# Six planned layers of a Trainium2 kernel: unread identity products where the planner expects TensorE to wait, and the delta rule's output in two groups of products

## The chip, the cores and the metric

The kernel runs on one core of one Trainium2 chip. The time is the device time of one execution in microseconds, from runs without the profiler; the profile is one further execution, taken by the hardware profiler. The core's engines are TensorE (PE in the profile, with its weight loads as PEld), VectorE (DVE), ScalarE (ACT), GpSimd (POOL) and SyncE (SP), which issues transfers. TensorE reads SBUF and writes PSUM[...].

## The reference

Eight sub-layers, each added to the residual stream x after a layer norm. x has 8 sequences of 256 positions and 128 channels in the kernel's layout.

```python
for f in (gated_delta_rule, windowed_attention_ffn, plucker_attention,
          ternary_ffn, flash_attention, mixture_of_experts,
          bidirectional_mamba, int8_ffn):
    x = x + layernorm(f(layernorm(x)))
```

The change touches the first of them most. Its core, for each of 16 heads with 64 key and 128 value channels, is the recurrence

```python
S = S * exp(g_t)                      # S: 64 x 128 a head
delta = (v_t - k_t @ S) * b_t
S = S + outer(k_t, delta)
o_t = (q_t * 64 ** -0.5) @ S
```

after which o is normed, gated and projected. Everything is fp32.

## The kernel before

**The delta rule in chunks.** `l0_attn` works on units of one sequence and eight heads (two units a sequence, 16 in all), each cut into two chunks of 128 positions, c = 0 and c = 1. For each chunk `prepare` makes scaled and transposed keys and queries, `decays` the decay factors E, `products` the matrices M (keys with keys) and, in E's place, the masked products of queries and keys. `inverse` inverts the triangular matrices of the eight heads by levels, in products of 64x64 tiles (L739 to L812) with evacuations between them. `outputs` forms what remains. Its output step is at L859 to L867: in a PSUM tile of 128 x 2 x 512 fp32 each head h has a region of 128 columns, at bank r = h // 4 and place p = h % 4. L863 adds `Q[:, h, :]` times `dl[:, h, :]` (128 contraction rows, inside the chunk); for c = 1, L865 adds `T2` times the state `St` that chunk 0 left (64 contraction rows: heads of r = 0 in the lower half of the partitions, those of r = 1 in the upper). The two alternate, head by head. After the step, L870 squares the result on ScalarE. L826, earlier in `outputs`, multiplies another half of `T2` with the same `St`, all eight heads in one go.

**The planner.** The first six layers are written as tasks, each a Python generator that yields between steps. `Turns.run` keeps a clock for each engine and a price for each instruction, and each time takes the step that could start first; so the order in which the instructions of all six layers are issued is fixed by the planner's clock when the program is built. On the chip an engine takes its instructions in that order and waits by semaphores. A step that names "ps" in its `yield` needs one of four PSUM slots (`ps`, 4 KB a partition each[...]) and two classes of SBUF slots (`4k`, `2k`, 25 each). `S.leave` gives a slot back to the planner at the step's planned end.

Parts that the change reads:

- `issued` is called for every instruction; it prices it, moves `clock[engine]` and `now`. For TensorE, `matmul` does so: 1.7 ns a column for fp32, 0.85 for a transpose, 0.43 for bf16; `tiles` holds when each 32x32 tile of the array is free, and a change between half and whole rows or columns (`mode`) waits for all of them and 150 ns (`SWITCH`).
- `starts` remembers, for each step of each generator's code, on which engine its first instruction ran when the step was first met.
- `ready`, set in `run`, is the time at which the step's task and its slots are ready in the planner's clock.
- `ps()` takes the PSUM tile for a step; nearly all of the 54 calls stand right before the step's first product.
- `k.ident16` is the identity in bf16, used before in the mask products of L670, L1081 and L1348, which multiply it with a mask repeated over 512 or 256 columns.

**After the six layers** come the Mamba layer `l3_attn` and the last FFN `l3_ffn`, in an order written out by hand. They start with L1898 and use neither the planner nor its slots.

The tile framework makes an instruction wait for the last readers of a buffer that it writes. A product's instruction, and any ahead of it in TensorE's queue that writes the same slot, therefore waits until the slot's last reader is done.

Some names in the profile: `Z` and `XY` are the inverse's tiles (L763; L339 and L341 are `evac` on ScalarE and VectorE), `E` in L863 is `Q`, `S` is `St`, `T` is `T2` there.

Of the kernel before, what the change touches and what calls it, by code (L numbers as in the profile page):

```python
# [16 lines left out]
P = 128  # L17
# [145 lines left out]
class Ctx:  # L163


    def __init__(self, tc, I, es):
        self.tc, self.nc, self.I = tc, tc.nc, I
        self.const = es.enter_context(tc.tile_pool(name="const", bufs=1))
        self.small = es.enter_context(tc.tile_pool(name="small", bufs=8))
        self.turn = 0  # L170
# [96 lines left out]
def over(ap, n, axis):  # L267

    a = ap.unsqueeze(axis)
    s = list(a.shape)  # L270
    s[axis] = n
    return a.to_broadcast(s)


class Turns:
# [2 lines left out]

    HOP, SWITCH = 150.0, 150.0

    def __init__(self, k, es, slots):
        self.nc = k.nc
        self.pools = {
            c: es.enter_context(k.tc.tile_pool(name="turns_" + c, bufs=n, **({"space": PSUM} if c == "ps" else {"side": "right"})))
            for c, n in slots.items()
        }
        self.slots = {c: [0.0] * n for c, n in slots.items()}
        self.clock, self.starts, self.users = {}, {}, {}  # L290
        self.tables = self.mode = None
        self.tiles = {}
        self.tasks = []
        self.now = self.queue = 0.0

    def add(self, name, after, steps):
        self.tasks.append((len(self.tasks), list(after), name, steps))
# [32 lines left out]
        return self.pools[c].tile(shape, F32, name=name, tag=c)  # L330

    def ps(self):
        return self.tile("ps", [P, 2, 512], "ps")

    def evac(self, out, in_):

# [34 lines left out]
    def issued(self, ins):  # L371

        e, op = str(ins.engine), ins.opcode
        aps = [a for a in list(ins.outs) + list(ins.ins) if hasattr(a, "bass_ap")]
        if not aps or "DMA" in op or "SP" in e:
            return
        n = max(self.size(a) for a in aps)
        if "PE" in e:
            self.matmul(ins, aps)
            return  # L380
        elif "Pool" in e:
            t = 350.0 + (1.6 if n > 64 else 160.0 if "pow" in str(getattr(ins, "op", "")) else 2.0) * n
        elif "Act" in e:
            t, f = 190.0 + 0.83 * n, str(getattr(ins, "func", ""))
            table = next((x for x in ("Silu", "Gelu", "Sqrt") if x in f), "Exp" if "Exp" in f or "Tanh" in f else self.tables)
            if table != self.tables:
                self.tables, t = table, t + 1283.0
        else:
            t = (165.0 if op != "TensorScalarPtr" else 205.0) + 1.03 * n
        start = max(self.clock.get(e, 0.0), self.ready if e == self.engine else self.now + self.HOP)  # L390
        self.clock[e] = start + t
        self.now = max(self.now, start + t)
        self.first = self.first or (e, None)
        self.engine = e

    def run(self):
        ends, live, todo = {}, [], self.tasks
        self.tasks = []
        hook = self.issued
        self.nc.push_inst_callback(hook)  # L400
        while live or todo:
            for task in [t for t in todo if all(a in ends for a in t[1])]:
                todo.remove(task)
                order, after, name, steps = task
                live.append([order, max([ends[a] for a in after], default=0.0), {}, name, steps, 0])
            best = None
            for task in live:
                order, ready, needs, _, steps, at = task
                if any(len(self.slots[c]) < n + spare for c, (n, spare) in needs.items()):
                    continue  # L410
                for c, (n, _) in needs.items():
                    ready = max(ready, sorted(self.slots[c])[n - 1])
                engine, mode = self.starts.get((steps.gi_code, at)) or (None, None)
                free = self.clock.get(engine, 0.0)
                if mode:
                    free = max([free] + list(self.tiles.values())) + self.SWITCH * (mode != self.mode)
                key = (max(ready, free), order)
                if best is None or key < best[0]:
                    best = key, ready, task
            assert best, [(t[3], t[2]) for t in live]  # L420
            _, ready, task = best
            for c, (n, _) in task[2].items():
                for i in range(n):
                    self.slots[c].remove(min(self.slots[c]))
            self.now = self.ready = ready
            self.engine = self.first = None
            needs = next(task[4], self)
            self.starts.setdefault((task[4].gi_code, task[5]), self.first)
            task[5] += 1
            if needs is self:  # L430
                live.remove(task)
                ends[task[3]] = self.now
            else:
                task[1], task[2] = self.now, {}
                for c in (needs or "").split():
                    c, _, spare = c.partition("+")
                    n, most = task[2].get(c, (0, 0))
                    task[2][c] = n + 1, max(most, int(spare or 0))
        self.nc.remove_inst_callback(hook)
# [24 lines left out]
def l0_attn(k, S, before, soon):  # L464
# [12 lines left out]
    nc, x, sm = k.nc, k.x, k.sm  # L477
    R2, H4, C2 = range(2), range(4), range(2)
    HALF = (slice(0, 64), slice(64, 128))
# [27 lines left out]
    def gates(n):  # L507

        yield "2k+5 ps"
        gt = gts[n] = S.tile("2k", [P, 7, 4, 16], "gates")  # L510
        ps, xT = S.ps(), xTs[n]
        beta, g, eG, eGd, z, u, acc = (gt[:, i] for i in range(7))
        for j in H4:
# [16 lines left out]
        nc.vector.scalar_tensor_tensor(g, acc, -1.0, over(k.l0a_alog, 4, 1), ALU.mult, ALU.mult)  # L530
        yield "ps"
        ps, gf = S.ps(), g.rearrange("p i h -> p (i h)")
        nc.tensor.matmul(ps[:, 0, 0:64], k.upto, gf, start=True, stop=True)
        nc.tensor.matmul(ps[:, 0, 64:128], k.ones, gf, start=True, stop=True)
# [282 lines left out]
    def outputs(h2, b, c):  # L817
        heads = "p r (s t) -> p (r s) t"
        v, Q, Yf, T2, xT = vs[h2, b][c], Es[h2, b, c], Yfs[h2, b, c], T2s.get((h2, b)), xTs[b // 2]
        if c:  # L820
            St = Ss[h2, b]
            yield "ps"
            ps = S.ps()
# [7 lines left out]
        ps = S.ps()  # L831
# [3 lines left out]
        dl = S.tile("4k", [P, 8, P], "dl")  # L835
        S.evac(dl.rearrange("p h t -> p (h t)"), ps.rearrange("p r c -> p (r c)"))
        S.leave("ps")
        if c == 0:
            yield "ps"
            ps = S.ps()  # L840
# [4 lines left out]
            St = Ss[h2, b] = S.tile("2k", [P, 4, P], "S")  # L845
# [4 lines left out]
        ps = S.ps()  # L850
# [7 lines left out]
        S.leave("ps")  # L858
        yield "ps"  # L859
        ps = S.ps()  # L860
        for h in range(8):
            r, p = divmod(h, 4)
            nc.tensor.matmul(ps[:, r, p * P:(p + 1) * P], Q[:, h, :], dl[:, h, :], start=True, stop=c == 0)  # L863
            if c:
                nc.tensor.matmul(ps[:, r, p * P:(p + 1) * P], T2[HALF[r], 0, p, :], St[HALF[r], p, :], start=False, stop=True)  # L865
        if c:
            S.leave("4k", "2k")  # L867
        yield
        osq = Q
        nc.scalar.activation(osq.rearrange("p h t -> p (h t)"), ps.rearrange("p r c -> p (r c)"), AF.Square)  # L870
# [12 lines left out]
        ps = S.ps()  # L883
# [31 lines left out]
    for n in H4:  # L915
        add(("n", n), before(n) + [own("x", 2 * n - 4)] * (n > 1), normed(n))
        add(("g", n), [own("n", n)], gates(n))
        for b in (2 * n, 2 * n + 1):

            add(("y", b), [own("n", n)] + [own("x", b - 3)] * (b > 2), room_for(b))  # L920
            for h2 in R2:
                u = 2 * b + h2
                prev = [own("o", (u - UNITS) % 2, (u - UNITS) // 2, 0)] if u >= UNITS else []
                add(("p", h2, b), [own("n", n), own("y", b)] + prev, project(h2, b, 0))
                for c in C2:
                    add(("r", h2, b, c), [own("p", h2, b), own("g", n)], prepare(h2, b, c))
                    add(("d", h2, b, c), [own("r", h2, b, c)], decays(h2, b, c))
                    add(("m", h2, b, c), [own("d", h2, b, c)], products(h2, b, c))
                for c in C2:
                    add(("i", h2, b, c), [own("m", h2, b, c)], inverse(h2, b, c))  # L930
                add(("v", h2, b), [own("m", h2, b, 1)], project(h2, b, 2))
                for c in C2:
                    after = [own("i", h2, b, c), own("v", h2, b)] + [own("o", h2, b, 0)] * c + [own("o", 0, b, c)] * h2
                    add(("o", h2, b, c), after, outputs(h2, b, c))
            add(("x", b), [own("o", h2, b, c) for h2 in R2 for c in C2], result(b))
# [1296 lines left out]
```

## Time and profile before

| | us |
|---|---|
| median of 3 runs (lowest to highest) | 4478.55 (4474.95 to 4483.94) |
| the profiled execution's own time | 4480.55 |
| its span, first to last instruction | 4478.8 |

| engine | busy us | share of the span | instructions |
|---|---|---|---|
| PE | 3675.4 | 82% | 54864 |
| PEld | 2916.3 | 65% | 54864 |
| DVE | 2973.7 | 66% | 4244 |
| POOL | 2723.5 | 61% | 2023 |
| ACT | 2582.6 | 58% | 4531 |

A view by stretch gives the busy time of each engine between two times. The granted clock is the share of TensorE's full clock that the throttle let through, a mean over the stretch. A group's line gives its kernel line, engine, operation, what it writes and reads by tile names, and how many; a source view adds shortest, median and longest duration in ns. Ends of products are modelled, so from one start to the next is the safer measure of what one costs. A wait's line says which engine's instruction waited for which, with the total, the number of waits and the longest. In a timeline, the brackets hold the idle time before an instruction and what ended it.

### The profile page before, as it was taken

Reading aid. Unit: us, or ns where it says so; the run is one execution under the profiler, and the core shown is the slowest. Engines: PE = TensorE matmul, PEld = TensorE weight load, DVE = VectorE, ACT = ScalarE, POOL = GpSimd, SP = SyncE. Lnnn points to the kernel's source line nnn. Section 1 sums busy time; section 2 is a strip of 40 time slices with the busy share of each in tenths; the row PEclk is TensorE's granted clock in tenths of the full one; section 3 lists DMA queues with packets and bytes.
Section 4 is the critical chain, followed back from the end, with each engine's and each line's share of the span. In section 5 each row is a group of like instructions: output and inputs, shape, how many; then the busy total and the mean of one; then the engine's idle time right before and its main releaser. Section 6 shows DMA issues by size and latency. Waiting matters only on the chain. (4 is left out here: it accounts for less than half of the span.)

```text
span 4478.8 us, 124521 instructions
## 1 busy us (share of the span) xinstructions
PE 3675.4 (82%) x54864; PEld 2916.3 (65%) x54864; DVE 2973.7 (66%) x4244; ACT 2582.6 (58%) x4531; POOL 2723.5 (61%) x2023
## 2 busy tenths in 40 slices
PE   5888888787888887889998987578887887888886
PEld 4676677676776665556555555367776876777774
DVE  6565666555556565663346676659888987987995
ACT  3434444444434454554434544388978887898883
POOL 5564556647555444441123334569988987988993
PEclk8989989898999988998898988789989999999997
DMA  1000000000000000000000000023323332333331
GB/s 54 3 2 2 3 2 3 2 2 2 9 21 3 20 11 5 8 23 15 6 1 1 5 1 1 10 79 106 100 89 95 106 98 82 105 101 89 104 111 30
DMA packets 98676, 168.86 MB, mean 38 GB/s; under 512 B 16699, under 2 KB 26582, under 8 KB 98006
## 3 DMA queue, kind: packets, MB, share of 16 engines
q1 hardware_dynamic: 98134, 160.89, 12.1%
q8 instruction: 431, 7.06, 0.6%
q14 instruction: 111, 0.91, 0.1%
HBM read 153.51 MB, written 2.10 MB: 35 GB/s over the span
## 5 line engine op out<-in xcount | busy, mean ns | idle before, releaser
L2069 POOL TENSOR_TENSOR hc<-h,Cs 128x1024 f32<-128x1024 f32 x480 | 1127.7, 2378 | 123.1 <-DVE h L2067 112.7
L2067 DVE TENSOR_TENSOR_SCAN h<-dA,ps_h 128x1024 f32<-128x1024 f32 x480 | 1069.7, 2271 | 122.7 <-PE ps_h L2061 39.0
L2046 ACT ACTIVATE dA<-dt,A 128x512 f32<-128x512 f32 x1024 | 684.7, 714 | 176.3 <-DVE h L2067 150.8
L2079 PE MATMUL ps_y<-w_c_ident,hc 128*128 128x128 f32 x4096 | 569.0, 283 | 131.7 <-POOL hc L2069 102.6
L2079 PEld LDWEIGHTS ps_y<-w_c_ident,hc 128*128 128x128 f32 x4096 | 462.2, 144 | 185.1 <-POOL hc L2069 175.7
L2043 ACT ACTIVATE sT<-dtxT,B 128x256 f32<-128x256 f32 x1024 | 451.3, 495 | 4.3 <-PE ps_h L2061 4.3
L569 DVE SCALAR_TENSOR_TENSOR acc<-ps,w_l0a_conv,acc 128x253 f32<-128x253 f32 (+2 forms) x768 | 310.6, 471 | 76.1 <-ACT acc L563 76.0
L2059 PE MATMUL ps_h<-dB,dtxTt 64*64 64x64 f32 x16384 | 305.5, 225 | 45.2 <-DVE h L2067 34.6
L2059 PEld LDWEIGHTS ps_h<-dB,dtxTt 64*64 64x64 f32 x16384 | 270.0, 138 | 99.2 <-DVE h L2067 46.3
L2061 PE MATMUL ps_h<-w_c_ident,sT 128*128 128x128 f32 x2048 | 280.5, 282 | 61.3 <-DVE h L2067 35.8
L2061 PEld LDWEIGHTS ps_h<-w_c_ident,sT 128*128 128x128 f32 x2048 | 241.8, 146 | 79.1 <-DVE h L2067 32.9
L721 POOL TENSOR_TENSOR Ps<-M,w_c_levels 128x512 f32<-128x512 f32 x192 | 240.6, 1272 | 85.9 <-DVE M L695 83.0
L339 ACT COPY XY<-ps 128x1024 f32<-128x1024 f32 (+1 forms) x132 | 124.5, 948 | 249.9 <-PE ps L786 235.6
L220 POOL TENSOR_SCALAR ln_rs<-ln_mv 128x4 f32<-128x4 f32 (+1 forms) x84 | 21.0, 251 | 397.9 <-DVE ln_mv L218 334.8
L779 PE MATMUL ps<-Z,XY 64*64 64x64 f32 x4608 | 188.7, 238 | 65.8 <-DVE Z L763 58.4
L779 PEld LDWEIGHTS ps<-Z,XY 64*64 64x64 f32 x4608 | 158.0, 148 | 84.1 <-DVE Z L763 45.1
L786 PE MATMUL ps<-XY,Z 64*64 64x64 f32 x5120 | 187.6, 237 | 4.0 <-issue 4.0
L760 PE MATMUL ps<-XY,Ps 64*64 64x64 f32 x5120 | 121.2, 234 | 75.2 <-DVE gate L880 15.9
L786 PEld LDWEIGHTS ps<-XY,Z 64*64 64x64 f32 x5120 | 164.8, 149 | 3.4 <-issue 3.4
L760 PEld LDWEIGHTS ps<-XY,Ps 64*64 64x64 f32 x5120 | 102.7, 144 | 92.2 <-issue 59.2
L563 ACT ACTIVATE acc<-ps,w_l0a_conv 128x256 f32<-128x256 f32 x256 | 100.2, 474 | 99.5 <-PE ps L557 80.6
L763 DVE TENSOR_TENSOR Z<-ps,w_c_ident 128x512 f32<-128x512 f32 x160 | 107.4, 683 | 73.0 <-PE ps L760 72.2
(456 smaller groups left out, 8716.8 us busy)
## 6 DMA issues: line engine op xcount, KB each, us to landing
Cs<-cd SPq DMA_DIRECT2D x512, 256.0 KB, 3.3
dtxTt<-dtxT SPq DMA_DIRECT2D x32, 128.0 KB, 3.9
wk<-in_l0a_w SPq DMA_DIRECT2D x8, 256.0 KB, 5.2
w_h<-in_l1f_h SPq DMA_DIRECT2D x4, 512.0 KB, 5.2
w_l2a<-in_l2a_w SPq DMA_DIRECT2D x3, 512.0 KB, 3.6
w_l0a_wg<-in_l0a_wg SPq DMA_DIRECT2D x1, 1024.0 KB
w_qk<-in_l0f_wqkv SPq DMA_DIRECT2D x2, 512.0 KB, 3.7
cv<-in_l3a_m_conv SPq DMA_DIRECT2D x2, 512.0 KB, 4.2
```

Of the source, the lines that this page charges most:

```text
L569: nc.vector.scalar_tensor_tensor(acc[:, n, s:L], p4[:, n, 0:L - s], conv[:, h2, 4 * j + n, 3 - s:4 - s], acc[:, n, s:L], ALU.mult, ALU.add,)
L721: nc.gpsimd.tensor_tensor(t, M[:, :, 0:64], over(k.l0a_levels[:, n, :], 8, 1), ALU.mult)
L760: nc.tensor.matmul(ps[to, a, at(j)], Ps[own, h, :], XY[own, t, at(i)], start=True, stop=True)
L779: nc.tensor.matmul(ps[own, a, at(j)], XY[rows, t, at(i)], Z[rows, za, at(zj)], start=True, stop=True)
L786: nc.tensor.matmul(ps[to, a, at(4 + j)], Z[rows, za, at(zj)], XY[rows, t, at(i)], start=True, stop=True)
L2043: nc.scalar.mul(st["s"][:, j], o["dtxT"][:, j], o["B"][:, j, n:n + 1])
L2046: nc.scalar.activation(dA[:, :, ec, :], by_seq(o["dt"][:, ec, :]), AF.Exp, scale=w["A"][:, ec, n:n + 1])
L2059: nc.tensor.matmul(ps[q, b, ec, j * 64:(j + 1) * 64], o["dtxTt"][rows, j, ec, q], dB[rows, j, :], start=True, stop=True)
L2061: nc.tensor.transpose(ps[:, j // 2, ec, j % 2 * P:(j % 2 + 1) * P], st["s"][:, j, ec, :], k.ident)
L2067: nc.vector.tensor_tensor_scan(h.rearrange(flat), st["dA"].rearrange(flat), st["in"].rearrange(flat), 0.0, ALU.mult, ALU.add)
L2069: (nc.vector if on_v else nc.gpsimd).tensor_tensor(st["hc"], h, over(by_seq(st["C"]), 2, 2), ALU.mult)
L2079: nc.tensor.matmul(o["py"][:, 2 * b + j, ec, :], st["hc"][:, b, ec, j * P:(j + 1) * P], k.ident, start=first, stop=n == N - 1, is_transpos ...
```

## The change

Two edits.

`Turns.ps`: before a step runs, `run` now notes in `expected` the engine that `starts` holds for it. If that is TensorE, `ps` computes how long TensorE would wait in the planner's clock, from the end of its last planned product to `ready`. For each 220 ns of it beyond 1500 ns (`IDLE`) it emits one bf16 product of the identity with the identity repeated four times, 128 x 512, into the first bank of the tile just taken. Nothing reads it; the step's own products write over it. While these are emitted `filling` is set, and `issued` leaves them out of the planner's clock.

`outputs`: for c = 1 the eight products of L865 now come first, in one group, place by place and the two row halves beside each other; then the eight products of L863. The accumulation flags change with it: a bank is started by its first product only, and `S.leave` of the two tiles moves up to stand between the groups.

```diff
-    HOP, SWITCH = 150.0, 150.0
+    HOP, SWITCH, IDLE = 150.0, 150.0, 1500.0
...
-        self.nc = k.nc
+        self.nc, self.k = k.nc, k
...
+        self.filling = False
...
     def ps(self):
-        return self.tile("ps", [P, 2, 512], "ps")
+
+
+        ps = self.tile("ps", [P, 2, 512], "ps")
+        if self.expected == "EngineType.PE":
+            gap = self.ready - max([self.clock.get("EngineType.PE", 0.0)] + list(self.tiles.values()))
+            self.filling = True
+            for _ in range(int((gap - self.IDLE) / 220.0)):
+                self.nc.tensor.matmul(ps[:, 0, :], self.k.ident16, over(self.k.ident16, 4, 1), start=True, stop=True)
+            self.filling = False
+        return ps
...
-        if not aps or "DMA" in op or "SP" in e:
+        if self.filling or not aps or "DMA" in op or "SP" in e:
             return
...
             self.engine = self.first = None
+            self.expected = (self.starts.get((task[4].gi_code, task[5])) or (None,))[0]
             needs = next(task[4], self)
...
         ps = S.ps()
+        if c:
+            for p in H4:
+                for r in R2:
+                    nc.tensor.matmul(ps[:, r, p * P:(p + 1) * P], T2[HALF[r], 0, p, :], St[HALF[r], p, :], start=p == 0, stop=False, skip_group_check=True)
+            S.leave("4k", "2k")
         for h in range(8):
             r, p = divmod(h, 4)
-            nc.tensor.matmul(ps[:, r, p * P:(p + 1) * P], Q[:, h, :], dl[:, h, :], start=True, stop=c == 0)
-            if c:
-                nc.tensor.matmul(ps[:, r, p * P:(p + 1) * P], T2[HALF[r], 0, p, :], St[HALF[r], p, :], start=False, stop=True)
-        if c:
-            S.leave("4k", "2k")
+            nc.tensor.matmul(ps[:, r, p * P:(p + 1) * P], Q[:, h, :], dl[:, h, :], start=c == p == 0, stop=True, skip_group_check=True)
         yield
```

## The prediction

> **What bounds the kernel now.** I read three views in this order: the page's slices, busy time by stretch, and the groups and waits of TensorE. The last product of the six planned layers starts at 2887.45 us (timeline of PE), so I cut the span there.
>
> ```profile
> 0.00:2888.00 2888.00, 2401.09 (x31360) 1807.02 (x31360) 1666.29 (x3348) 1282.28 (x2168) 1362.79 (x1319) 0.90 0.03 8
> 2888.00:4478.80 1590.80, 1274.33 (x23504) 1109.33 (x23504) 1307.44 (x896) 1300.32 (x2363) 1360.67 (x706) 0.94 0.31 92
> ```
>
> The columns after the length are PE, PEld, DVE, ACT, POOL busy, granted clock, DMA. In the first stretch PE is busy for 83% and the next engine (DVE) for 58%: TensorE bounds it, with 472 us of idle in 270 gaps over 0.15 us, which I added up from the trace. The second stretch (the Mamba layer and the last FFN, on POOL at 86%) is not touched by the change; I take its 1591 us as fixed.
>
> The granted clock of 0.90 is a mean over two states. In these windows around one idle time (same columns, width first) it is 1.00 or 0.50:
>
> ```profile
> 437.60:441.00 3.40, 3.40 (x53) 2.79 (x56) 3.40 (x9) 1.44 (x4) 3.40 (x3) 1.00 0.00 0
> 441.00:444.40 3.40, 0.71 (x50) 0.57 (x40) 1.36 (x4) 1.14 (x2) 3.23 (x3) 1.00 0.00 0
> 444.40:447.80 3.40, 0.00 (x0) 0.00 (x0) 2.22 (x5) 0.00 (x0) 3.40 (x4) 0.50 0.00 0
> 447.80:451.20 3.40, 1.27 (x47) 1.30 (x50) 3.40 (x7) 0.00 (x0) 3.40 (x4) 0.50 0.02 5
> 451.20:454.60 3.40, 2.99 (x50) 2.80 (x45) 3.40 (x9) 0.00 (x0) 3.40 (x4) 0.50 0.00 0
> 454.60:458.10 3.50, 3.50 (x110) 3.07 (x109) 3.50 (x10) 1.99 (x2) 2.57 (x3) 1.00 0.02 5
> ```
>
> One window with PE busy for 0.71 of 3.40 us is followed by half clock; it goes only after a window with 2.99. Over the record of the clock up to 2888 us I counted 80 half-clock periods, 597 us in all, with PE busy for 466 us of them. The window before such a period was busy for less than half in 69 cases; of 583 windows at full clock that stayed there, 3 were. Products stretch in proportion: two 128x512 bf16 products with the identity start 0.216 us apart at full clock, 0.427 at half. At full clock the 466 us would take 233: that is all there is to win from the clock.
>
> **Part 1: the output with grouped products.** For the second half of a sequence (c = 1) L863 and L865 alternate, 8 products each, and an fp32 product is two instructions:
>
> ```profile
> L865 PE MATMUL ps<-S,T x256: 272/373/579, 198.4 to 1548.5; 64*128 64x128 f32 x128
> L826 PE MATMUL ps<-S,T x256: 272/272/373, 185.1 to 1528.4; 64*128 64x128 f32 x128
> ```
> ```profile
> 284.23 0.49 PE L865 MATMUL ps<-S,T 64*128 64x128 f32 x2
> 284.65 0.49 PE L863 MATMUL ps<-dl,E 128*128 128x128 f32 x2
> 285.07 0.48 PE L865 MATMUL ps<-S,T 64*128 64x128 f32 x2
> ```
>
> Each pair takes 0.42 us, so the block 16 x 0.41 = 6.6 us (15 of the 16 blocks, 6.3 to 6.7 from first start to the next step; one, at half clock, 11.6). L826 is the same 8 products of 64 rows, already grouped: its block takes 1.09 us, two row halves at a time. The 8 products of L863 alone (c = 0) take 1.79 to 1.95. After the change 1.09 + 1.9 = 3.0, saving 3.6 x 16 = **58 us** of PE. Bounds: 21 if the 64-row products didn't overlap (16 instructions x 0.21 + 1.9 = 5.3), 62 with the cold block's larger share. I take 58; the L826 row is the same form and order.
>
> How much of PE time reaches the end? PE is 83% busy in this stretch and its idle times wait for others, so a gain is partly eaten by the next wait. Bounds 0.3 and 1; I take 0.75, a little under the busy share, for gains and losses alike. 58 x 0.75 = **44 us**.
>
> **Part 2: the identity products.** The planner adds them where its own clock expects TensorE to wait over 1.5 us, one for each 0.22 us beyond that. The planned waits are not in the trace, so I use the real ones: 98 gaps over 1.5 us, 348 us, of which 201 lie beyond the 1.5. At 0.22 us that is some 900 products; bounds none and twice as many, since the plan is not the run.
>
> *What they bring.* If each of these gaps kept only 1.5 us, the window before a half-clock period would be busy for over 55% in all but 9 or so, leaving 61 of 597 us. So at best 536 x 0.78 (466/597) / 2 = 209 us of PE time. The plan will hit some waits and miss others; between 0 and 209 I take two thirds, 139, as the planner's prices agree with the rows (it counts 218 ns for an fp32 product of 128 columns, two instructions of 109 to 112 here). 139 x 0.75 = **104 us**.
>
> Here a rule stands against the change. The Trainium skill, page "TensorE: Matmul & The Clock Gate", Part 1 on the HAM clock gate, puts the ramp penalty under 1% of a typical kernel's span, and its closing table warns only of idle gaps over some 3 us. By the first all this would be worth at most 45 us; by the second (a window of 3.41 us) 35 gaps count, and only 34 of the 80 periods have one next to them: 34/80 x 233 = 99 us. The trace has 233/4479 = 5.2% of the span, and windows with several shorter waits that turn the clock too. The rows decide; by the rules the term of 104 would be 22 to 49 (times 2/3 and 0.75).
>
> *What they cost.* A fill writes the PSUM slot that its step has just been given, so it can't start before that slot is free. Look at what ended the longest of the example's waits:
>
> ```profile
> 449.93 1.13 PE L760 MATMUL ps<-XY,Ps 64*64 64x64 f32 x32 [8.22 <-DVE v L828]
> ```
>
> L760 reads XY and Ps, not v; L828 reads a PSUM slot and frees it. In such a gap the fill begins when the products could have begun: its whole length is delay. By the releaser's names 35 of the 98 gaps are of this kind, with 63 us beyond 1.5. The other gaps, 138 us beyond 1.5, wait mostly for their own data:
>
> ```profile
> PE ps L779 <- DVE Z L763: 58.4, 31, 7.2
> PE ps L760 <- DVE gate L880: 15.9, 5, 4.8
> PE ps L760 <- ACT XY L339: 13.2, 6, 5.1
> PE ps L1644 <- POOL e L1635: 13.0, 7, 5.1
> ```
>
> The second line is a slot again (L760 reads no gate); in the other three the fill lies in the wait and costs nothing, if the wait is there. Where the third that misses falls, the 1.5 us margin covers about half: 138 / 3 / 2 = 23. Paid: 63 + 23 = 86 us, x 0.75 = **64 us**; bounds 0 and 201 x 0.75 = 151. Queued behind a late fill is every later product of PE, and behind those the evacuations on DVE and ACT that free the next slot.
>
> *The order.* Part 1 shortens steps in the plan's clock, so all later choices of the planner can change. Nothing in the profile prices this; I take 0 with 15 us either way. The fills change no choice, since they are left out of the plan's clock.
>
> **Sum.** -44 - 104 + 64 = -84 us. The profiled execution took 4480.55 us (span 4478.8, 1.75 around it): 4480.6 - 84 = 4396.6. It was 2.0 above the median of the three runs, so **4395 us** on their scale, 1.9% faster.
>
> **The rivals.**
>
> *The plan is good* (0.22): the waits are where the planner expects them and slots are free, so fills cost nothing. (58 + 209) x 0.75 = 200 us: 4278. For it: the planner's prices fit; most of the gap time waits for data. Against it: the 35 gaps on slots.
>
> *The fills land on the path* (0.15), the slower side. Place: the head of a step's products, in order on PE. The skill's same page, Part 2 on what happens when a matmul is issued, says that the matmuls stay in program order and only weight loads are pulled ahead; no row here shows a product passing another, so a fill can't be overtaken. With all 201 us paid and a third of the clock's gain (70): (201 - 58 - 70) x 0.75 = +55: 4533. It decides once the paid fills exceed what grouping and the clock give, 128 us with that clock. For it: a static plan against an execution whose waits depend on the clock itself; at half clock a fill takes twice its planned time.
>
> *Another limit takes over* (0.14): the chains of the inverse (Z, XY on DVE and ACT) keep the step rate and only 0.3 of the PE time passes: (58 + 139 - 86) x 0.3 = 33: 4445. For it: with 111 us less work PE would be busy for 79% only, and L779 waits for Z 31 times already. Against it: no other engine exceeds 58%.
>
> *The fills don't hold the clock* (0.07), so the change doesn't do what it says: products of the identity are mostly zeros, and before has only 256 such instructions (L670, L1081, L1348), each beside other products. Grouping stays, the fills are paid: -44 + 64 = +20: 4498.
>
> The likeliest has 0.42. **Range**: the likeliest alone spans about 4340 to 4450 (order, share passed, hits); reaching halfway into the first rival and into the slower ones gives 4270 to 4515, with some 0.2 left out. A change within 0.2% (9 us) can't be told from none here: the three runs lie 9 us apart. Faster: 0.40 + 0.22 + 0.13 and a little of the last two cases = 0.78; same 0.03; slower 0.19.
>
> **What would show it.** Grouping: c = 1 blocks of about 3.0 us, ScalarE's wait for L865 (93.0 us in 16 waits) nearly gone. Clock: granted clock up to the end of the sixth layer at 0.96 or more, half-clock time under 250 us. Fills: some 900 products of the identity into ps under the new line; their busy time mostly where PE was idle. Path: the first stretch ends near 2804 us. Wrong if the clock rises and the stretch doesn't shorten (other limit), if the clock stays at 0.90 (not held), or if steps start later after their fill than their data was ready (on the path).

## The result, and the profile after

| | before | after |
|---|---|---|
| median of 8 runs each | 4477.73 us | 4465.23 us |
| ratio, with its 95% interval | 1 | 0.9969 (0.9960 to 0.9978) |
| profiled execution (span) | 4480.55 (4478.8) | 4469.94 (4468.1) |

By the medians the changed kernel is 12.5 us faster; by the ratio of the runs it is 0.31%, or 14 us. The forecast had the sign right and the time lies in its range, but its own figure was 84 us.

The busy times by stretch of the changed kernel, cut at the end of its sixth layer (columns: length, PE, PEld, DVE, ACT, POOL, granted clock, DMA share, GB/s):

```profile
0.00:2875.40 2875.40, 2400.20 (x31761) 1781.37 (x31761) 1664.95 (x3341) 1282.62 (x2173) 1360.24 (x1316) 0.91 0.03 8
2875.40:4468.10 1592.70, 1274.37 (x23504) 1109.34 (x23504) 1307.43 (x896) 1300.36 (x2363) 1361.95 (x707) 0.94 0.31 92
```

The second stretch is what it was, so all of the gain is in the first: 2887.9 to 2875.4 us. The striking number is TensorE's busy time: 2401.1 before, 2400.2 after. The real products shrank, as meant, and the identity products took up all the time that they left. They are these, in the source view of the new line (count, duration in ns, first and last start):

```profile
L341 PE MATMUL ps<-ident x401: 376/379/634, 39.6 to 2861.6; 128*128 128x512 bf16 x134
```

(The x134 at the end is the count of shapes in every third of them.) They number 401, not 900. Without them TensorE's busy time would be 2297 us, so they add 103 us; its idle time went from 487 to 475. Half-clock time, by the record of the clock, went from 597 to 495 us and the granted clock from 0.90 to 0.91, not to 0.96.

The output step does what it was to do. From the timeline of the changed kernel (start, length, engine, line, what, count):

```profile
196.44 1.16 PE L875 MATMUL ps<-S,T 64*128 64x128 f32 x16
197.53 2.05 PE L879 MATMUL ps<-dl,E 128*128 128x128 f32 x16
199.52 0.27 PE L790 MATMUL ps<-Z,XY 64*64 64x64 f32 x2
```

From the first start to the next step 3.08 us, against 6.6 before. ScalarE's waits for the output step (L870, both chunks) fell from 103 to 47 us, so they are halved and not nearly gone. The delta rule's layer as a whole ended at 1529.2 instead of 1567.8 us: 38.6 us earlier, of which only 12.5 were left at the end of the sixth layer. So something was lost behind it; the run with the new order alone, below, shows how much.

Where the fills went is seen in single places. Three from the timeline of the changed kernel (in brackets the idle time before, and what ended it):

```profile
504.85 2.33 PE L341 MATMUL ps<-ident 128*128 128x512 bf16 x10
...
509.16 0.27 PE L790 MATMUL ps<-Z,XY 64*64 64x64 f32 x2 [1.98 <-DVE Z L774]
...
1692.72 3.66 PE L341 MATMUL ps<-ident 128*128 128x512 bf16 x9 [4.50 <-ACT e L1112]
1696.21 0.60 PE L1176 MATMUL ps<-w_c_ident,h 128*128 128x128 f32 x4
...
2470.19 11.60 PE L341 MATMUL ps<-ident 128*128 128x512 bf16 x53
2482.31 1.94 PE L1340 MATMUL ps<-w_c_ident,lp 128*128 128x128 f32 x16 [0.51 <-DVE l L1636]
```

The first is as planned: the fill runs at once, and the wait for Z still outlasts it by 1.98 us. The second is late: TensorE stood still for 4.50 us until the slot was free, then ran nine products, and the step's transposes, which do not read `e`, followed without a pause. The third holds TensorE for 11.6 us: 53 products stand for a planned wait of at least 13.2 us (53 x 0.22 + 1.5), and the wait that is left is 0.51 us, not the planned 1.5. Sorting all 47 places so: in 7, with 17 us of fills, a wait was left after the fill; in 25, with 48 us, TensorE had already waited and the product followed at once; in 15, with 41 us, fill and product both ran at once, so that the fill just covered its wait or overran it, which the trace can't tell. (The 113 us of an expectation below are the same fills, counted up to the start of the next product.)

### The profile page after: what moved, and what is told of

The parts are those of the page before. It is cut to its first block, busy times and chain, and to the rows that moved or that the text cites. A ratio compares the mean times of both kernels' runs of the same rounds, so it can differ in the third digit from the quotient of the medians.

```text
span 4468.1 us, 125288 instructions
## 1 busy us (share of the span) xinstructions
PE 3674.6 (82%) x55265; PEld 2890.7 (65%) x55265; DVE 2972.4 (67%) x4237; ACT 2583.0 (58%) x4536; POOL 2722.2 (61%) x2023
## 5 line engine op out<-in xcount | busy, mean ns | idle before, releaser
L580 DVE SCALAR_TENSOR_TENSOR acc<-ps,w_l0a_conv,acc 128x254 f32<-128x254 f32 (+2 forms) x768 | 313.9, 473 | 56.2 <-ACT acc L574 55.9
L2071 PE MATMUL ps_h<-dB,dtxTt 64*64 64x64 f32 x16384 | 305.6, 225 | 44.8 <-DVE h L2079 34.3
L341 PE MATMUL ps<-ident 128*128 128x512 bf16 x401 | 111.0, 428 | 61.5 <-DVE qn L1067 19.3
```

The costliest lines, as they stand in the source:

```text
L580: nc.vector.scalar_tensor_tensor(acc[:, n, s:L], p4[:, n, 0:L - s], conv[:, h2, 4 * j + n, 3 - s:4 - s], acc[:, n, s:L], ALU.mult, ALU.add,)
L2071: nc.tensor.matmul(ps[q, b, ec, j * 64:(j + 1) * 64], o["dtxTt"][rows, j, ec, q], dB[rows, j, :], start=True, stop=True)
```

## The experiments

Ratios are to before, on the same chip, with a 95% interval; 1% is 44.8 us. To keep an order of instructions while the products change, the output's products are issued in one order and priced by the planner in the other: while `S.held` below is a list, `issued` only collects in it, and afterwards it is called in the order that is to be priced. I state three theories: **order** (the planner's new order lost the gain), **late fills** (the fills fall on the path), and **another limit** (TensorE's time doesn't carry through). Stretches of profiles run from the start to the end of the sixth layer.

**Grouping alone, in the order of before.**

```diff
+        S.held = []
+        if c:
+            for p in H4:
...
+        held, S.held = S.held, None
+        inner = held[-8:]
+        for h in range(8):
+            r, p = divmod(h, 4)
+            S.issued(inner[h])
             if c:
...
+                S.issued(held[2 * p + r])
```

> Grouped products alone, every instruction in the order of before (the plan is priced as if the products still alternated). In the changed kernel the delta rule's layer ended 38.6 us earlier (1567.8 to 1529.2) and the whole kernel only 12.5. Theory 'order': grouping passes on most of its 58 us of TensorE time when the order stays, and the new order of the later layers lost it: 35 to 55 us faster than before. Theory 'another limit': TensorE's time does not carry through, whatever the order: under 18 us faster. Theory 'late fills': as the first, 35 to 55, since the loss is the fills' own.

0.9938 (0.9919 to 0.9956), 28 us faster. Between the theories: more than "another limit" allows, less than the others. 28 of 58 us reach the end here. One stretch of its profile (of the slowest of its six runs):

```profile
0.00:2872.40 2872.40, 2364.03 (x31360) 1791.85 (x31360) 1667.21 (x3348) 1282.23 (x2168) 1362.87 (x1318) 0.89 0.03 8
```

TensorE's busy time fell by 37 us only, as products ran at half clock for 502 us against 466, and its idle time grew by 22.

**Grouping alone, planned anew.** The change without `ps` and `filling`.

> Grouped products alone, planned anew, so in the order of the changed kernel but without its identity products. 'Order': no better than the changed kernel, 5 to 20 us faster than before. 'Late fills': 30 to 55 us faster, so taking the fills out of the changed kernel makes it faster by 20 to 40. 'Another limit': under 18 us faster.

0.9973 (0.9964 to 0.9981), 12 us. The same products, 16 us slower than in the old order, with intervals that don't meet; and level with the changed kernel (0.9960 to 0.9978). So the order matters, and the 401 fills bring nothing on top that can be told from zero.

**Fills alone**, the change without the grouping:

> The identity products alone, in the plan of before, which they do not change. In the changed kernel 401 of them take 113 us of TensorE, and in 40 of 47 places the products follow a fill at once, so nothing was left to wait for. 'Late fills': they cost more than the clock returns: 5 to 40 us slower than before. 'Order' and 'another limit': within 10 us of before.

0.9986 (0.9979 to 0.9993), 6 us faster: 343 fills. Late fills as the only cause would have made it slower; in that form the theory falls.

**Fills where the profile of before shows the waits.** The planner's gap is replaced by a table from the trace: for each call of `ps`, the idle time before its first product, if that ended with the step's own data; one product for each 0.216 us beyond 1.5.

```diff
+        self.filling = True
+        for _ in range(FILLS.get(self.count, 0)):
+            self.nc.tensor.matmul(ps[:, 0, :], self.k.ident16, over(self.k.ident16, 4, 1), start=True, stop=True)
+        self.filling = False
+        self.count += 1
```

> Identity products not where the plan expects waits but where the profile of before showed them, and only where the wait ended with the step's own data (48 places, 495 products, each wait filled up to its last 1.5 us); order of before, products still alternating. By the record of the clock this should take away some 42 of 80 half-clock periods, 362 us of half clock, 146 us of TensorE time. 'Late fills' (the place is what failed): 40 to 110 us faster. 'Another limit': the clock rises by some 0.04 over the six layers, the time falls by under 20 us. 'Order' says nothing of it beyond that it should gain.

0.9978 (0.9970 to 0.9987), 10 us faster. Half-clock time fell to 437 us and the clock rose to 0.92, but the time hardly moved. That spoke for "another limit".

**The same 495 products where TensorE does not wait.**

> The same 48 fills with 495 products (107 us at 0.216) as the run filled by the profile, but each moved to a step of before at which TensorE had no wait and which lies as far from one as can be found nearby; order of before, no grouping. It gives the price of TensorE time by itself. 'TensorE bounds': nearly all of it passes, 80 to 107 us slower. 'Chains bound' (steps that pass from engine to engine set the pace and TensorE's idle time gives way): 0.4 of it, as grouping in the old order passed on some 24 to 28 of 58: 25 to 55 us slower.

1.0188 (1.0172 to 1.0205), 84 us slower: 0.79 of 107 passes. As a limit that keeps TensorE's time from showing at all, "another limit" is refuted. One stretch of its profile:

```profile
0.00:2979.50 2979.50, 2493.78 (x31855) 1851.78 (x31855) 1673.87 (x3348) 1284.08 (x2168) 1363.27 (x1318) 0.91 0.03 8
```

PE is busy for 93 us more than before, and idle for 486 us, as before (487): the time just adds up. Half-clock time is 560 us, 37 less than before; in the run above, with as many products, it was 160 less. So for the clock, too, the place counts.

**Fills at the waits for a slot** (31 places, 278 products, by the same table):

> Fills by the profile of before at the other kind of wait: 31 places, 278 products (60 us), where the wait ended with another step's reading of PSUM, so with the slot that the fill needs. No grouping, order of before. 'Late fills', as the prediction had it: the whole length is delay, 0.75 of 60: 40 to 60 us slower. 'Chains bound': 0.4 of 60 less what the clock returns: between 5 faster and 25 slower.

1.0081 (1.0066 to 1.0096), 36 us slower, 0.6 of the 60 us. In 29 of its 31 places TensorE had waited before the fill and the product followed at once. A fill behind a slot delays its step, and what it costs is shown; the prediction would have said 45.

```profile
0.00:2930.80 2930.80, 2455.55 (x31638) 1814.59 (x31638) 1669.84 (x3348) 1283.25 (x2168) 1363.61 (x1318) 0.90 0.03 8
```

The 278 products take 94 us here, as many run at half clock after the wait. The real products are 39 us shorter than before, so the balance is 55 us more of TensorE.

**Both edits in the order of before.**

> Both edits of the change, but with the plan of before (grouping not priced), so the changed kernel without its new order. If the two edits add up: 24 to 28 from grouping and 6 to 9 from the fills, 30 to 37 us faster than before. If both live on the same idle time: no better than grouping alone. If the new order had nothing to do with the loss: 12 us faster, as the changed kernel.

0.9951 (0.9936 to 0.9966), 22 us faster: no better than grouping alone (28, intervals overlap). That the 6 us of the fills add to it is not seen.

**The 58 us put on VectorE instead.**

```diff
+        if c:
+            S.mute = True
+            for _ in range(3):
+                nc.vector.tensor_reduce(rs, osq, AX.X, ALU.add)
+            S.mute = False
         nc.vector.tensor_reduce(rs, osq, AX.X, ALU.add)
```

While `mute` is set, `issued` leaves them out of the planner's prices; the three make the same row sums each time.

> Grouping in the old order, which took 58 us from TensorE, and the same 58 us put on VectorE one step later in the same chain: the row sums after a c = 1 output are made four times instead of once (48 reductions of 1.22 us, kept out of the plan's prices). 'TensorE bounds': VectorE is busy for 58% of the six layers, so nothing of it shows: as grouping alone, 20 to 28 us faster than before. 'Chains bound': a chain does not care which engine holds it: 20 to 58 us slower than grouping alone, so at the time of before or above it.

1.0018 (1.0010 to 1.0025): 36 us slower than grouping alone, 0.6 of 58.

```profile
0.00:2896.40 2896.40, 2361.63 (x31360) 1790.14 (x31360) 1724.38 (x3396) 1282.60 (x2168) 1362.39 (x1318) 0.89 0.03 8
```

VectorE was busy for only 58% of the stretch before, and yet time put on it at this step passes nearly as time on TensorE does; TensorE's idle time grew from 508 us to 535, its busy time did not. I read it so: no engine alone bounds the six layers, steps that pass from one to the next do. One step was tried, and some 50 instructions of GpSimd also stand elsewhere in this run, so for other steps it is argued.

**Half the products at the measured waits** (the table's counts halved):

> As the run filled by the profile at the waits for own data, with half the products at each place (46 places, 235 products, some 51 us), so each measured wait keeps half of what lies beyond 1.5 us as margin. If fills that overrun their wait ate the clock's gain there: 15 to 35 us faster than before. If the clock is worth little in any case (the freed time turns into idle time): no more than the full fill's 8 to 10 us.

0.9923 (0.9904 to 0.9941), 34 us faster, against 10 with all of them. The two stretches, half first, then all:

```profile
0.00:2855.80 2855.80, 2418.23 (x31595) 1792.74 (x31595) 1661.95 (x3348) 1281.29 (x2168) 1362.13 (x1317) 0.92 0.03 8
```
```profile
0.00:2883.80 2883.80, 2463.63 (x31855) 1801.27 (x31855) 1669.28 (x3348) 1282.60 (x2168) 1363.55 (x1319) 0.92 0.03 8
```

The clock is 0.92 in both: half the products hold it nearly as well (464 us of half clock, against 437), and TensorE is busy for 45 us less. Sorted as above, fills after which no wait was left take 85 us with all of them and 39 with half. So even at measured waits, filling all but 1.5 us was too much. Part of that is the slot again: in 21 places of the full run, with 59 us of fills, TensorE had waited before the fill, although the wait of before had ended with the step's own data. Who ended a wait does not tell when the slot was free.

**The order alone**: before with one price changed by 1 ns.

```diff
-    HOP, SWITCH = 150.0, 150.0
+    HOP, SWITCH = 149.0, 150.0
```

> The kernel of before with the planner's price of a hand-over between engines at 149 ns instead of 150: the same work, another order. If the order alone is worth the 11 to 16 us that lie between grouping in the old order and grouping planned anew: such runs lie some 5 to 20 us off before, either way. If order is worth nothing: within 4 us.

> The same with 151 ns. Again 5 to 20 us off before if the order matters, within 4 if not.

149 ns: 0.9946 (0.9931 to 0.9961), 24 us faster. 151 ns: 1.0053 (1.0039 to 1.0067), 24 us slower. The same products, and nearly twice the effect of the change either way. (An evacuation goes to ScalarE or VectorE by the planner's clock: of 672, a net six move to ScalarE at 149 ns, two at 151 and seven in the change's new order; ScalarE's table loads, 185 before, are 186, 171 and 181. The slowest of these has the fewest, so they don't explain it.) The stretches, 149 first:

```profile
0.00:2860.10 2860.10, 2378.26 (x31360) 1790.53 (x31360) 1675.27 (x3342) 1281.91 (x2175) 1363.14 (x1318) 0.91 0.03 8
```
```profile
0.00:2914.00 2914.00, 2424.23 (x31360) 1813.36 (x31360) 1689.47 (x3346) 1259.79 (x2156) 1359.06 (x1318) 0.89 0.03 8
```

All three orders have 31360 products. TensorE's idle time is 482, 487 and 490 us; its busy time is 2378, 2401 and 2424, and the half-clock time 533, 597 and 655. Products ran at half clock for 408, 466 and 515 us of it; with that counted as half, the busy times are 2174, 2168 and 2167. So in these two the order moved the time mostly by how long the products ran at half clock.

**Grouping with half fills at its own measured waits**, old order:

> Grouping in the old order with half fills at the waits for own data that the trace of that kernel shows (49 places, 247 products). If well-placed short fills add to grouping: 35 to 55 us faster than before, the best so far. If the idle time gives way to whatever is saved: as grouping alone, 24 to 28 us.

0.9905 (0.9888 to 0.9922), 43 us faster. That is 15 more than grouping alone, with intervals that just meet (0.9922 and 0.9919), and less than the 34 that half fills gave on before.

With these, three things were open: the new order's own price, whether fewer fills would help the changed kernel, and whether grouping gains the same elsewhere.

**The new order with the old products**: priced as grouped, issued alternating.

> The order of the run with grouping planned anew, instruction for instruction, with the products of the output alternating as in before and no identity products. If the new order is a worse one by itself and grouping is worth some 24 to 28 in any order: 8 to 20 us slower than before. If the order is neutral and grouping is worth only 12 in it: within 5 us of before.

1.0069 (1.0054 to 1.0085), 31 us slower than before, more than either theory gave. Set beside the run with grouping in the very same order (0.9973), new order first:

```profile
0.00:2917.00 2917.00, 2403.62 (x31360) 1801.93 (x31360) 1661.38 (x3341) 1282.53 (x2171) 1361.58 (x1317) 0.90 0.03 8
```
```profile
0.00:2874.80 2874.80, 2346.25 (x31360) 1775.16 (x31360) 1660.03 (x3341) 1281.55 (x2171) 1360.35 (x1317) 0.89 0.03 8
```

57 us less of TensorE, and 43 us less of time (1.0069 - 0.9973 = 0.0096). The new order costs TensorE 27 us of idle time more than before's (513 against 487), at nearly the same busy time. By the last products of a layer it is 9 us behind before at the end of the delta rule (1576.9 against 1567.8), 61 behind at the end of the second layer (2201.6 against 2140.3), and 29 at the end of the sixth.

**The changed kernel with half its fills** (a divisor of 440 in place of 220, 189 products).

> The changed kernel with one product for each 440 ns of a planned wait beyond 1.5 us, so 189 products in place of 401. If overrun ate the gain, as at the profile's own waits: 15 to 30 us faster than the changed kernel, 27 to 42 faster than before. If the plan's places are what is wrong (26 of 88 real waits over 1.5 us are among its 60): within 6 us of the changed kernel.

0.9961 (0.9949 to 0.9972), 4 us faster than the changed kernel, with overlapping intervals. Where the plan puts the fills, fewer of them are no remedy.

**Grouping in the order of 149 ns.**

> Grouping in the order that the price of 149 ns gave, which alone was 24 us faster than before. If grouping's share of 0.4 to 0.5 is general: 22 to 30 us more, 46 to 54 faster than before. If gains that lower TensorE's time do not add up: 24 to 35 faster.

0.9886 (0.9873 to 0.9900), 51 us faster than before: 27 more than that order alone. It is the fastest of the runs, 37 us below the changed kernel by the ratios, with no fills at all.

**And half fills at its measured waits on top:**

> The order of 149 ns with grouping, and half fills at the waits for own data that its own trace shows (38 places, 207 products). If they add up as half fills did on before (34 us): some 80 us faster than before. If as on grouping in the old order (28 to 44, so 15 more): 60 to 70. If its idle time gives nothing more: 53, as without fills.

0.9885 (0.9869 to 0.9902): nothing more.

## Why the prediction was wrong

The runs split the 12.5 us into three (each a difference of ratios, times 4479 us, so that they add up to the 14 of the ratio):

| term | predicted | measured |
|---|---|---|
| grouping, in the new order | -44 | 0.9973 - 1.0069: -43 (35 to 51 less) |
| the new order itself | 0, 15 either way | 1.0069 - 1: +31 (24 to 38) |
| identity products, clock less cost | -104 + 64 = -40 | 0.9969 - 0.9973: -2 (some 6 either way) |
| sum | -84 | -14 |

**What bounds the kernel** was half right. TensorE's time does pass, at 0.79 when it is added on purpose, close to the 0.75 that I took. But I read "83% busy, the next engine 58%" as one engine with slack beside it; 58 us on VectorE passed at 0.6. The busy shares are averages over steps that wait for one another.

**Part 1, grouping,** was right: 3.6 us a block as read from L826, and 43 us of 44 in the new order. In the other two orders it gave 28 and 27, so the share that passes is 0.46 to 0.74, by order. That 0.75 met it is in part luck: in the old order the half clock took back some of what was saved.

**The order** is the first step that failed: "Nothing in the profile prices this; I take 0 with 15 us either way." It cost 31. The bound was a guess: a price changed by 1 ns moves the time by 24 us, up or down. It was also not quite so that "the fills change no choice". By the code the planner's picks are the same with and without them, but in the runs with fills some instructions of VectorE, ScalarE and GpSimd stand elsewhere, in some 30 to 120 places, and on TensorE at times one step. How much of any fill's result is that shift was not separated, so the -2, and the distance between half and all fills at measured waits, may hold some of it.

**The clock** is the second, and its size: "between 0 and 209 I take two thirds, 139". With grouping planned anew, real products took 2346 us; with the fills 2297: 49 us. The plan did not hit two thirds of the waits. In the run with the same order and no fills, TensorE waited for over 1.5 us 113 times, with 216 us beyond that; 25 of the 47 places with fills are among them, with 60 us: 0.28 of the wait time. (In the order of before it is 24 of 52 places, and 55 of 201 us.) The argument that "the planner's prices agree with the rows" was about single durations; what the traces show is that the plan's waits and the chip's are largely in different steps. How the plan drifts off was not followed.

**The cost of the fills**: fewer than estimated, 401 for 900, as the plan expects fewer waits than the chip had, and 103 us of TensorE rather than 201. The mechanism, a fill that waits for its slot, was right and is seen in 25 places and in the run on slot waits. What was wrong is how often: 86 of 201 us were to be paid, and of 106 us in the sorting 48 delayed their step and up to 41 more did. Against the same order without fills, the 103 us stand in place of 49 us of shorter products and 53 us of idle time (529 to 475), and the six layers end at the same time: 2874.8 without, 2875.4 with them.

**The rule weighed against the change**, from the page "TensorE: Matmul & The Clock Gate" of the Trainium skill, Part 1, is that the ramp costs under 1% of a span. The page says it of the ramp at a kernel's start, and the prediction set it against many ramps. It would have put the clock's term at 22 us, so the fills' net at +42; by the rows it was -40, and -2 was measured, between the two. That half clock can cost far more here is not refuted by the -2: the run with 235 products at measured waits had 133 us less of it and was 34 us faster. What failed is the share of it that I granted the plan.

**The rivals**: "the fills land on the path" described most fills, but its clock and count were off and grouping outweighed it. "Another limit" came nearest in time (4445), but not by its cause: it let 0.3 of TensorE's time pass, and 0.79 did when added, 0.46 to 0.74 when grouping took it away. That steps on other engines share the path, as it said, the run on VectorE bears out. "The fills don't hold the clock" is refuted: half-clock time fell by 113 us against the same planning without fills.

## What to carry to other kernels

When an edit changes what a planner sees, its new order is a change of its own: price it by keeping the old order with the new instructions, and the new order with the old ones. A single comparison within 0.5% says little of an edit in such a kernel, as long as 1 ns in a price moves the time by as much.

Work that is to fill a wait needs the wait from a measurement and a wide margin: it is paid for where the wait is shorter, or where the filler itself waits for the resource (here a PSUM slot) that ends the wait. The margin here: half of each wait beyond 1.5 us filled gave 34 us, all of it 10.

## What the runs showed of the hardware

- Products of the bf16 identity, almost all zeros, hold TensorE's clock: half-clock time went from 608 us to 495 with 401 of them, and from 597 to 464 with 235 at measured waits. 495 where TensorE did not wait took it to 560 only, and a new order alone, without any, to 533 or 655.
- Alternating fp32 products of 64 and 128 contraction rows (128 columns) cost 6.6 us for 8 and 8; the same in two groups 3.1 us (1.09 and 1.99), at full clock.
- Products issued right after a wait run at half clock often: 158 of the 278 fills at waits for a slot did, and the 278 took 94 us where 60 were counted at full clock; of the 495 where TensorE did not wait, none did.
